# Starting a four-layer graph network kernel: filler products, an earlier flag and an earlier branch

## The chip, the core and the metric

The kernel runs on one core of a Trainium2 chip. A core has a matrix engine (TensorE, PE in the profile; its weight loads are listed as PEld), a vector engine (VectorE, DVE), an activation engine (ScalarE, ACT), a general one (GpSimd, POOL), and SyncE (SP), whose queue here issues all transfers between the chip's main memory and the core's on-chip memory (SBUF). Matrix products land in PSUM, which this kernel divides into eight banks of 128 x 512 fp32. Each engine works through its own list of instructions in order and waits on semaphores for the others.

The metric is device time in microseconds (us), as the median of several runs; smaller is better. One further execution is profiled.

## The reference

There are 32 graphs of 512 nodes with 128 features each, and one 512 x 512 adjacency matrix of zeros and ones that all graphs share. Four layers follow each other, each one of the form x = x + f(relu(layernorm(x))):

```python
# layer 0: attention (h is the normalized input)
x_h = elu(h @ Wi + bi)
e = sigmoid(x_h @ We[H:] [:, :, None] + (x_h @ We[:H])[:, None, :] + be)
e = e * (adj + 0.005 * (adj == 0))
recv = concat([einsum('bij,bjh->bih', e, x_h), x_h * sum(e, -1)]) @ Wn + bn
out = concat([elu(recv), x_h]) @ Wm + bm
# layer 1: five steps of a gated update, with adj as both matrices
m = adj @ h;  z, r = sigmoid(...), sigmoid(...);  h = (1 - z) * h + z * tanh(...)
# layer 2: adj @ (h @ weight) + bias
# layer 3: sum over k of adj^k @ h @ weight_k, up to the third power
```

All values are fp32.

## The kernel before

The kernel is one long list of operations that a planner puts in order before anything runs. `Plan.op` records an operation with its engine, an assumed duration, a due time, the buffers that it reads and writes, and a function that emits its instructions. `Plan.order` then goes through an assumed timeline: whenever an engine comes free it takes the ready operation with the earliest due time, if buffers are free, and if the operation isn't due more than 60 us behind the oldest one left. The emitted order on each engine is what the plan found; the hardware adds the real waits.

Buffers are kinds with slots: "f" (36 tiles of 128 x 512), "q" (4 such tiles in the rounded format fp32r), "s" (small statistics), "x" (input and running sum of four graphs each), "b" (the eight PSUM banks), and "m" and "d" (blocks in main memory, through which token-major and feature-major layouts are exchanged).

A product of fp32 operands is shown in the trace as two matmul records, one of fp32r operands as one. Products with the adjacency matrix can run in fp32r only if rounding leaves every adjacency value unchanged. So the kernel counts the values that rounding changes (`inexact`), reads that count into a register of each engine (L906), and branches (L907) to one of two arms, which hold everything that was not ordered before. In the arm taken here (`arm(True)`), the adjacency `A_r` is fp32r and the tokens are split into two fp32r parts.

What stands before the branch is what `plan.order(end=BRANCH)` places in the first 30 us of its own timeline:

- Loads on SP: graph 0, `Wi`, the four row blocks of the adjacency (`A_nat`), then small weights, biases and graphs 1 to 3 (L279, L295).
- For graph 0 to 3: layer normalization (L434 to L447), PE transposes (L334), the copy out of PSUM (L394), the product with `Wi` (L405, a helper's line), exp, tanh and relu for elu on ACT (L492, L410, L495), its two combining steps on DVE (L497, L499), the products with `W_tok` (L521), attention ends spread by transposes (L558), tanh of each of four tiles (L572) and their masking on DVE (L575), and the products with the messages (L583).
- The adjacency: 16 PE transposes (L464), the rounding copy `A_r` (L466) and a scaled copy (L468) on ACT, the mask (L469) and the comparison of `A_r` with the transposed original (L472) on DVE, which leaves counts in `n_odd`; PE sums these over the partitions (L479), and DVE writes the integer flag `inexact` (L484).

After the branch, SP loads the weights of the later layers; DVE, PE and ACT go on with the first graphs; PE makes the weight transposes (L674) and the adjacency in a permuted order of columns (L757, with a permuted identity called `swap`). Row sums of the masked tiles are taken with a matrix of ones (L405 with `ones`), the node's own part is multiplied in (L609), and layer 0 ends with L619. The later layers' lines are L769 (tokens with adjacency), L405 with w3T, w4T, w5T, u3T, u5T (gates), L833 (layer 2), L850 and L859 (layer 3).

Due times come from constants: each graph begins `PACE` = 56 us after the one before, the first ones by `b * FIRST_PACE` with 10 us; graphs 4 and 5 have due times of 40 and 56.

Of the kernel before, what the change touches and what calls it, by code (L numbers as in the profile page):

```python
# [10 lines left out]
F32 = mybir.dt.float32  # L11
# [5 lines left out]
P = 128  # L17
# [21 lines left out]
class Plan:  # L39
# [7 lines left out]
    def __init__(self, slots, ahead, last):  # L47
        self.ahead, self.last, self.ops, self.vals = ahead, last, [], {}
        self.free = {k: [(0.0, i) for i in range(n)] for k, n in slots.items()}
        self.until = dict.fromkeys(self.RESULT, 0.0)  # L50
        self.shared, self.now = 0.0, 0.0

    def op(self, eng, us, due, emit, reads=(), writes=(), two=False, keep=0, result=None):

        o = Op(eng, us, self.RESULT[eng] if result is None else result, emit, two, keep)
        for v in reads:
            o.before.add(v.writer)  # L60
# [42 lines left out]
    def order(self, end=None):  # L103
# [9 lines left out]
        for i, o in enumerate(left):  # L113
            index[o] = i
            o.waits = sum(not b.begun for b in o.before)
            o.ready = max([0.0, *(self.known(b, o) for b in o.before if b.begun)])
            if not o.waits:
                heapq.heappush(coming[o.eng], (o.ready, i, o))
                events.append(o.ready)
# [16 lines left out]
        while events:  # L136
# [3 lines left out]
            for e in self.until:  # L140
# [12 lines left out]
                for x in passed:  # L153
                    heapq.heappush(ready[e], x)
                if o is None:
                    continue
# [29 lines left out]
def tile_four_graph_layers(  # L186
# [34 lines left out]

    PACE, FIRST_PACE, LAST_PACE = 56.0, 10.0, 30.0
    BRANCH = 30.0

# [25 lines left out]
    def at(v):  # L250
        if v.tile is not None:
            return v.tile
        return places[v.kind][v.slot] if v.whole is None else at(v.whole)[:, v.part]
# [13 lines left out]
    op("POOL", 1.0, -9, lambda: make_identity(nc, at(ident)), [], [ident])  # L267
    op("DVE", 0.2, -9, lambda: nc.vector.memset(at(ones), 1.0), [], [ones])
    op("POOL", 0.2, -9, lambda: nc.gpsimd.memset(at(neg_half), -0.5), [], [neg_half])
    ones_r = const("ones_r", [P, P], F32R)  # L270
# [6 lines left out]

    def load(v, src, due, us=0.5, to=None):
        op("SP", us, due, lambda: nc.sync.dma_start(at(v) if to is None else to(at(v)), src), [], [v])  # L279
        return v  # L280

    def load_const(src, shape, name, due, us=0.5):
        return load(const(name, shape), src, due, us)

# [9 lines left out]
    def load_graph(b, due):  # L294
        op("SP", 1.5, due, lambda: nc.sync.dma_start(  # L295
            at(X[b]), x[b].rearrange("(c p) d -> p c d", p=P)),
            [], [X_group[b // G], X[b]] if b % G == 0 else [X[b]])

    load_graph(0, -9)
    Wi_sb = load_const(Wi, [P, P], "Wi_sb", -9)  # L300
    A_nat = [Val("f") for _ in range(NC)]
    for ic in range(NC):
        load(A_nat[ic], adj[ts(ic, P), :], -8, 1.3)
    bi_sb = load_column(bi, "bi_sb", -8)

# [4 lines left out]
    be_sb = load_const(be.partition_broadcast(P), [P, 1], "be_sb", -7)  # L310
    load_graph(1, -6)
    Wn_sb = load_const(Wn[P:], [P, P], "Wn_sb", -6)
    bn_sb = load_column(bn, "bn_sb", -6)
    Wm_sb = load_const(Wm.rearrange("(t p) o -> p t o", p=P), [P, 2, P], "Wm_sb", -5)
    bm_bc = load_const(bm.partition_broadcast(P), [P, P], "bm_bc", -5)
    load_graph(2, -4)
    load_graph(3, -3)

# [139 lines left out]
    inexact = const("inexact", [1, 1], I32)  # L458
    n_odd = const("n_odd", [P, NC])
    for jc in range(NC):  # L460
        pt, z, odd = Val("b"), Val("f"), Val("f")
        def turn(jc=jc, pt=pt):
            for ic in range(NC):
                nc.tensor.transpose(at(pt)[:, ts(ic, P)], at(A_nat[ic])[:, ts(jc, P)], at(ident))  # L464
        op("PE", T_TR, jc, turn, [*A_nat, ident], [pt])
        op("ACT", T_COPY, jc, lambda jc=jc, pt=pt: nc.scalar.copy(at(A_r)[:, jc, :], at(pt)),  # L466
           [pt], [A_r])
        op("ACT", T_COPY, jc, lambda z=z, pt=pt: nc.scalar.mul(at(z), at(pt), 1 / ALPHA), [pt], [z])  # L468
        op("DVE", T_VEC, jc, lambda jc=jc, z=z, pt=pt: nc.vector.scalar_tensor_tensor(  # L469
            at(mask)[:, jc, :], at(pt), 0.0, at(z), op0=ALU.is_equal, op1=ALU.add),  # L470
            [pt, z], [mask])
        op("DVE", 0.7, 8, lambda jc=jc, pt=pt, odd=odd: nc.vector.scalar_tensor_tensor(  # L472
            at(odd), at(A_r)[:, jc, :].bitcast(F32), 1.0, at(pt),
            op0=ALU.mult, op1=ALU.not_equal, accum_out=at(n_odd)[:, jc : jc + 1]),
            [A_r, pt], [odd, n_odd])
    p_odd = Val("b")
# [169 lines left out]
    assert inexact.writer.begun  # L646
    common = plan.state()

    def arm(exact):
        with ExitStack() as stack:  # L650
            pool = stack.enter_context(tc.tile_pool(name=f"arm{exact:d}", bufs=1))
            plan.back_to(common)
            list_rest(exact, pool)
            issue(plan.order())
# [291 lines left out]
```

## Time and profile before

| what | value |
|---|---|
| median of 3 runs | 1705.13 us (1702.95 to 1705.34) |
| profiled execution | 1704.23 us |
| its span, first to last instruction | 1702.4 us |
| mean granted TensorE clock | 0.996 |
| PE busy | 1665.6 us (98%) |
| DVE busy | 1478.8 us (87%) |
| ACT busy | 1099.6 us (65%) |
| POOL busy | 377.3 us (22%) |

The span is what the trace covers; the execution's time is 1.8 us longer. Busy time is the union of an engine's instructions. Matmuls overlap in the records and their ends are modelled, so a full PE row doesn't say that every matmul runs at its best rate; the distance between starts does. The bracket at the end of a timeline row tells how long the engine had been idle, and what released it. "Issue" there means that the profile shows nothing that it waited for.

### The profile page before, as it was taken

The numbers are of one execution on the slowest core, as the hardware profiler recorded it, in microseconds if no ns is written. First come the engines' busy times: TensorE is split into PE (matmuls) and PEld (weight loads), VectorE is DVE, ScalarE is ACT, GpSimd is POOL, SyncE is SP. The second block draws the span as 40 slices with busy tenths as digits, with TensorE's granted clock in tenths as the row PEclk, the third lists the DMA queues.
The fourth block names the chain that finished last, engine by engine and source line by source line (L and its number), as shares of the span: only waits on it lengthen the run. The fifth ranks groups of instructions, "written<-read, shape, count | busy, mean of one in ns | idle before, by whom it ended". The sixth has DMA issues, their size and how long they took to land.

```text
span 1702.4 us, 21136 instructions
## 1 busy us (share of the span) xinstructions
PE 1665.6 (98%) x6521; PEld 1065.7 (63%) x6521; DVE 1478.8 (87%) x3325; ACT 1099.6 (65%) x2075; POOL 377.3 (22%) x301
## 2 busy tenths in 40 slices
PE   5999999999999999999999999999999999999998
PEld 3565555666666666665666665666666666666787
DVE  5789999999989998889989898899999888877842
ACT  5786767777666776566676666667576756655550
POOL 3231122312312222222212222122232221001210
PEclk8999999999999999999999999999999999999999
DMA  3122323253333332242333333333333323222302
GB/s 95 36 69 93 123 96 99 70 150 92 93 99 112 100 105 88 76 123 93 94 108 91 94 107 87 100 107 107 89 112 95 95 86 101 81 75 75 95 6 62
DMA packets 266873, 156.54 MB, mean 92 GB/s; under 512 B 75392, under 2 KB 235008, under 8 KB 266752
## 3 DMA queue, kind: packets, MB, share of 16 engines
q1 hardware_dynamic: 266752, 155.12, 30.9%
q8 instruction: 53, 0.87, 0.2%
q14 instruction: 68, 0.56, 0.1%
HBM read 82.25 MB, written 72.81 MB: 91 GB/s over the span
## 4 chain that ended last, share of the span: by engine, by line
PE 84%; DVE 8%; DMA 3%; ACT 3%; issue 2%; SPq 0%; POOL 0%; DVEq 0%; ACTq 0%; POOLq 0%
PE b L405 39%; PE b L769 18%; PE b L859 9%; PE b L850 6%; PE b L583 4%; PE b L619 3%; DMA f<-d 2%; PE b L521 2%; DVE f L575 2%; PE b L833 1%; DVE r L743 1%; PE b L606 1%; ACT f L447 1%; DVE f L794 1%; DVE f L346 1%
## 5 line engine op out<-in xcount | busy, mean ns | idle before, releaser
L394 ACT COPY f<-b 128x512 f32<-128x512 f32 x360 | 207.8, 585 | 151.6 <-PE b L769 105.8
L769 PE MATMUL b<-AQ,r 128*128 128x512 f32 x1024 | 304.4, 439 | 0.8 <-DVE r L743 0.8
L439 POOL TENSOR_TENSOR s<-s,nhalf 128x4 f32<-128x4 f32 x128 | 156.0, 1219 | 645.8 <-DVE s L437 610.1
L769 PEld LDWEIGHTS b<-AQ,r 128*128 128x128 f32 x1024 | 192.1, 188 | 90.5 <-issue 49.9
L794 DVE TENSOR_TENSOR f<-f,b 128x512 f32<-128x512 f32 x320 | 211.8, 677 | 20.4 <-PE b L405 16.5
L447 ACT ACTIVATE f<-x,s 128x128 f32<-128x128 f32 x512 | 210.1, 488 | 23.0 <-DVE s L442 22.7
L346 DVE STREAM_TRANSPOSE f<-f 128x512 f32<-128x512 f32 x244 | 204.6, 845 | 22.3 <-ACT f L447 21.7
L859 PE MATMUL b<-r,A_r 128*128 128x512 f32 x768 | 223.6, 426 | 0.0
L410 ACT ACTIVATE f<-f,b4w 128x512 f32<-128x512 f32 x160 | 115.4, 723 | 165.2 <-DVE f L794 164.7
L594 POOL TENSOR_TENSOR f<-f,f 128x512 f32<-128x512 f32 x84 | 130.9, 1559 | 307.3 <-DVE f L575 231.0
L405 PE MATMUL b<-f,u5T 128*128 128x512 f32 x320 | 163.9, 596 | 7.9 <-DVE f L801 7.8
L859 PEld LDWEIGHTS b<-r,A_r 128*128 128x128 f32 x768 | 139.0, 189 | 44.9 <-issue 23.0
L405 PE MATMUL b<-f,w4T 128*128 128x512 f32 x320 | 163.4, 593 | 0.2 <-ACT f L394 0.2
L405 PE MATMUL b<-f,u3T 128*128 128x512 f32 x320 | 163.0, 592 | 0.4 <-DMA f<-m 0.4
L405 PE MATMUL b<-f,w5T 128*128 128x512 f32 x320 | 162.8, 592 | 0.0
L405 PE MATMUL b<-f,w3T 128*128 128x512 f32 x320 | 162.5, 592 | 0.0
L769 PE MATMUL b<-A_r,r 128*128 128x512 f32 x512 | 151.8, 439 | 2.5 <-DVE r L743 2.5
L410 ACT ACTIVATE f<-b,b5w 128x512 f32<-128x512 f32 x160 | 109.2, 684 | 64.5 <-PE b L405 63.5
L743 DVE TENSOR_TENSOR r<-f,r 128x512 fp32r<-128x512 f32 x192 | 143.1, 749 | 8.2 <-ACT r L739 8.1
L850 PEld LDWEIGHTS b<-V,f 128*128 128x128 f32 x1024 | 130.5, 192 | 24.8 <-issue 20.6
L410 ACT ACTIVATE f<-f,b3w 128x512 f32<-128x512 f32 x160 | 115.2, 720 | 42.5 <-DVE f L794 41.6
L811 DVE TENSOR_TENSOR f<-f,f 128x512 f32<-128x512 f32 x160 | 114.7, 718 | 29.3 <-ACT f L410 28.7
(103 smaller groups left out, 2623.8 us busy)
## 6 DMA issues: line engine op xcount, KB each, us to landing
m<-f SPq DMA_DIRECT2D x244, 256.0 KB, 2.1
f<-m SPq DMA_DIRECT2D x184, 256.0 KB, 2.9
f<-m SPq DMA_DIRECT2D x240, 64.0 KB, 2.2
x<-in_x_dram SPq DMA_DIRECT2D x32, 256.0 KB, 3.1
out_dram<-x SPq DMA_DIRECT2D x32, 256.0 KB, 2.4
f<-d SPq DMA_DIRECT2D x28, 256.0 KB, 5.1
f<-in_adj_dram SPq DMA_DIRECT2D x4, 256.0 KB, 4.0
f<-in_L_gnn_weight_dram SPq DMA_DIRECT2D x2, 224.0 KB, 3.3
```

What stands on the lines that cost most here:

```text
L346: op("DVE", us, due, lambda: nc.vector.transpose(view_out(at(blocks)), view_in(at(src))), [src], [blocks])
L394: op("ACT", us, due, lambda: nc.scalar.copy(at(t), at(src)), [src], [t])
L405: nc.tensor.matmul(to, at(w), of, start=start, stop=stop)
L410: op("ACT", us, due, lambda: nc.scalar.activation(at(dst), at(src), AF.Tanh, bias=at(bias), scale=scale), [src, bias], [dst])
L439: op("POOL", 1.2, due, lambda: nc.gpsimd.tensor_tensor(stat(SCALE), stat(VAR), at(neg_half), op=ALU.pow), [s, neg_half], [s])
L447: nc.scalar.activation(at(h)[:, ts(c, P)], at(X[b])[:, c, :], AF.Relu, bias=stat(SHIFT)[:, c : c + 1], scale=stat(SCALE)[:, c : c + 1],)
L594: op("POOL", 1.4, d - 10, lambda: nc.gpsimd.tensor_tensor(at(dst), at(a), at(c), op=ALU.add), [a, c], [dst])
L743: op("DVE", T_VEC, due, lambda: nc.vector.tensor_tensor(part(lo), whole(), part(hi).bitcast(F32), op=ALU.subtract), [src, hi], [lo], two=two)
L769: nc.tensor.matmul(at(pa), at(part)[:, ts(jc, P)], view(at(columns)[:, jc, :]), start=jc == n == 0, stop=jc == NC - 1 and n == PARTS - 1,)
L794: op("DVE", T_VEC, d, lambda: nc.vector.tensor_tensor(at(s), at(u), at(pg), op=ALU.add), [u, pg], [s])
L850: nc.tensor.matmul(at(pz)[:, ts(i, D)], at(hT[i])[:, ts(ic, P)], at(V[k]), start=i == 0, stop=last and i == G - 1,)
L859: nc.tensor.matmul(at(pz), at(adjT)[:, jc, ts(ic, P)], at(part), start=False, stop=jc == NC - 1 and n == PARTS - 1,)
```

## The change

It has seven parts.

1. Filler. One PSUM bank (`spare`) is taken out of the plan up to the branch. Whenever PE has nothing ready on the planned timeline, a 128 x 128 product of `ones` with itself into that bank is emitted. Each is planned at 0.224 us, from 0.4 us on. Nothing reads the bank. After the branch it returns to the plan. The new kernel lists 52 such products: 31 first, then single ones between the adjacency's transposes, 15 behind the first `Wi` product, and 4 more.
2. The flag is counted from the adjacency as loaded: ACT rounds each row block into a "q" tile, and DVE compares that with the block; neither needs the transposes. The number of comparisons stays four.
3. The adjacency's remaining work gets other due times: transposes 8, scaled copies and masks 9 to 12, and the copies `A_r` 22.
4. Loads: graph 1 and `bi` move ahead of the adjacency, graph 2 right behind it, and `bm_bc` isn't issued before the branch. Planned durations of the large loads are smaller.
5. `BRANCH` is 18 in place of 30: fewer operations are placed ahead of the branch.
6. `FIRST_PACE` is 14 in place of 10; graphs 4 and 5 are due at 56 and 70.
7. Ahead of the branch the planner leaves an engine free for an operation that is due earlier and becomes ready within 0.3 of the candidate's duration.

```diff
+                if o is not None and end is not None and any(
+                    c.due < o.due and t < now + 0.3 * o.us for t, _, c in coming[e]
+                ):
+                    heapq.heappush(ready[e], (o.due, index[o], o))
+                    o = None
+                if o is None and e == "PE" and end is not None and self.idle.known <= now:
+                    order.append(self.idle)
+                    self.until[e] = now + self.idle.us
+                    heapq.heappush(events, self.until[e])
...
-    PACE, FIRST_PACE, LAST_PACE = 56.0, 10.0, 30.0
-    BRANCH = 30.0
+    PACE, FIRST_PACE, LAST_PACE = 56.0, 14.0, 30.0
+    BRANCH = 18.0
...
+    spare = places["b"].pop()
+    plan.free["b"].pop()
+    plan.idle = Op("PE", 0.224, 0.0, lambda: nc.tensor.matmul(
+        spare[:, :P], at(ones), at(ones), start=True, stop=True), False, 0)
+    plan.idle.known = 0.4
...
     load_graph(0, -9)
+    load_graph(1, -9)
     Wi_sb = load_const(Wi, [P, P], "Wi_sb", -9)
+    bi_sb = load_column(bi, "bi_sb", -9)
     A_nat = [Val("f") for _ in range(NC)]
     for ic in range(NC):
-        load(A_nat[ic], adj[ts(ic, P), :], -8, 1.3)
-    bi_sb = load_column(bi, "bi_sb", -8)
+        load(A_nat[ic], adj[ts(ic, P), :], -8, 0.65)
+    load_graph(2, -8)
...
-    load_graph(1, -6)
...
-    bm_bc = load_const(bm.partition_broadcast(P), [P, P], "bm_bc", -5)
-    load_graph(2, -4)
-    load_graph(3, -3)
+    bm_bc = load_const(bm.partition_broadcast(P), [P, P], "bm_bc", -5, earliest=BRANCH)
+    load_graph(3, -6)
...
+    for ic in range(NC):
+        short, odd = Val("q"), Val("f")
+        op("ACT", T_COPY, 9, lambda ic=ic, short=short: nc.scalar.copy(
+            at(short), at(A_nat[ic])), [A_nat[ic]], [short])
+        op("DVE", 0.7, 9, lambda ic=ic, short=short, odd=odd: nc.vector.scalar_tensor_tensor(
+            at(odd), at(short).bitcast(F32), 1.0, at(A_nat[ic]),
+            op0=ALU.mult, op1=ALU.not_equal, accum_out=at(n_odd)[:, ic : ic + 1]),
+            [short, A_nat[ic]], [odd, n_odd], two=True)
     for jc in range(NC):
-        pt, z, odd = Val("b"), Val("f"), Val("f")
+        pt, z = Val("b"), Val("f")
...
-        op("PE", T_TR, jc, turn, [*A_nat, ident], [pt])
-        op("ACT", T_COPY, jc, lambda jc=jc, pt=pt: nc.scalar.copy(at(A_r)[:, jc, :], at(pt)),
+        op("PE", T_TR, 8, turn, [*A_nat, ident], [pt])
+        op("ACT", T_COPY, 22, lambda jc=jc, pt=pt: nc.scalar.copy(at(A_r)[:, jc, :], at(pt)),
            [pt], [A_r])
-        op("ACT", T_COPY, jc, lambda jc=jc, pt=pt: nc.scalar.mul(at(z), at(pt), 1 / ALPHA), [pt], [z])
-        op("DVE", T_VEC, jc, lambda jc=jc, z=z, pt=pt: nc.vector.scalar_tensor_tensor(
+        op("ACT", T_COPY, 9 + jc, lambda z=z, pt=pt: nc.scalar.mul(at(z), at(pt), 1 / ALPHA), [pt], [z])
+        op("DVE", T_VEC, 9 + jc, lambda jc=jc, z=z, pt=pt: nc.vector.scalar_tensor_tensor(
             at(mask)[:, jc, :], at(pt), 0.0, at(z), op0=ALU.is_equal, op1=ALU.add),
             [pt, z], [mask])
-        op("DVE", 0.7, 8, lambda jc=jc, pt=pt, odd=odd: nc.vector.scalar_tensor_tensor(
-            at(odd), at(A_r)[:, jc, :].bitcast(F32), 1.0, at(pt),
-            op0=ALU.mult, op1=ALU.not_equal, accum_out=at(n_odd)[:, jc : jc + 1]),
-            [A_r, pt], [odd, n_odd])
...
     common = plan.state()
+    places["b"].append(spare)
...
             plan.back_to(common)
+            plan.free["b"].append((BRANCH, len(places["b"]) - 1))
```

Line numbers in the new kernel differ: L464 becomes L492, L472 becomes L484, L484 becomes L508, L521 becomes L545, L558 becomes L582, L572 becomes L596, L575 becomes L599, L583 becomes L607, L609 becomes L633, L757 becomes L783, L405 becomes L425, and L907 becomes L933. The filler is L285.

## The prediction

> **What bounds the kernel now.** First the page: the span, the busy times, and the rows over 40 slices.
>
> ```profile
> span 1702.4 us, 21136 instructions
> PE 1665.6 (98%) x6521; PEld 1065.7 (63%) x6521; DVE 1478.8 (87%) x3325; ACT 1099.6 (65%) x2075; POOL 377.3 (22%) x301
> PE   5999999999999999999999999999999999999998
> PEclk8999999999999999999999999999999999999999
> ```
>
> TensorE is the bound: it idles 36.8 us in 1702.4, and one slice, the first, is half empty and below full clock. Second, busy time by stage, cut where TensorE becomes continuous (47.35) and where its last matmuls begin. Columns: stretch, length, then PE, PEld, DVE, ACT, POOL busy with counts, granted clock, DMA share, GB/s.
>
> ```profile
> 0.00:47.35 47.35, 28.64 (x108) 17.76 (x109) 25.54 (x99) 29.07 (x62) 16.31 (x27) 0.86 0.31 85
> 47.35:1697.10 1649.75, 1636.58 (x6414) 1047.94 (x6413) 1451.82 (x3226) 1070.49 (x2014) 360.96 (x274) 1.00 0.31 92
> 1697.10:1702.40 5.30, 0.40 (x2) 0.00 (x0) 1.42 (x3) 0.00 (x0) 0.00 (x0) 0.97 0.51 148
> ```
>
> Idle: 18.7 at the start, 13.2 in the whole middle, 4.9 at the end. Finer cuts show the clock:
>
> ```profile
> 15.00:16.00 1.00, 0.00 (x0) 0.00 (x0) 0.47 (x1) 1.00 (x4) 1.00 (x1) 0.96 0.00 0
> 20.00:25.00 5.00, 4.39 (x24) 3.38 (x24) 1.87 (x9) 2.63 (x7) 1.64 (x2) 0.50 0.00 2
> 29.00:30.00 1.00, 1.00 (x3) 0.53 (x2) 0.00 (x0) 1.00 (x3) 0.95 (x1) 0.71 1.07 320
> ```
>
> Half speed runs from 15.9 to 29.6, and at the very start too, where no grant is recorded: the adjacency transposes take 0.213 each (3.41 for 16), later ones 0.11. Third, the timeline around the branch:
>
> ```profile
> 20.61 2.10 PE L521 MATMUL b<-W_tok,f 128*128 128x130 f32 x8 [7.46 <-DVE f L499]
> 23.36 0.14 DVE L484 CAST inexact<-b 1x1 int32<-1x1 f32 x1
> 32.39 0.69 DVE L497 SCALAR_TENSOR_TENSOR f<-f,f 128x512 f32<-128x512 f32 x1 [4.03 <-issue]
> 34.22 1.12 PE L583 MATMUL b<-f,f 128*128 128x512 f32 x2 [2.16 <-DVE f L499]
> ```
>
> The flag is written at 23.4-23.5. PE's branch instruction (L907) stands at 29.61 for 4.55 us; its next matmul starts at 34.22, though the DVE result that it needs was done at 28.35. DVE passes its branch at 28.10 and resumes at 32.39 (4.3), ACT takes 3.4 from its branch, and SP 3.66 from the flag to its next DMA (23.52 to 27.18).
>
> Now the work done in that start at full speed, with durations from later rows (0.43 per 128x512 fp32 record, two to a product; 0.11 per 128x128 or 128x130 record; 0.23 per 128x512 fp32r record). Before 47.35: 37 transposes by 0.11 and 8 of the attention ends (4.9 together), 4 Wi products 3.4, 24 W_tok records 2.6, eight L583 records 3.4, eight ones records 3.4, Wn 0.9, swap 0.9, count 0.2: about 19.9. So **27.4 us are lost by 47.35**: 18.7 idle, about 6.7 by half clock (13.4 busy us at half rate), 2 in small gaps. What follows is the same TensorE work in both kernels.
>
> **What the skill says.** "TensorE: Matmul & The Clock Gate", Part 1: the gate's default is half rate, and free-running windows of about 3.4 us decide. The trace agrees: full at 12.5, half from 15.9, full from 29.6, so steps of 3.41 and 13.65. A window with 0.65 busy of 3.41 lost the clock; one with about 2.2 kept it. "Runtime: NRT & Kernel Launch", Instruction fetch mechanics: a taken branch outside the fetched pages waits for a fetch; that fits the 3.4 to 4.6 us above. "Advanced Engine Details and Errata", Control Flow Timing, gives 0.108 us for a compare-and-branch; the trace's 4.55 decides.
>
> **The change, part by part**, in the order that the two built programs list.
>
> 1. Filler: 52 products of ones, 31 of them first (they need only the memset of ones, done at 0.98). Each has two 128x128 records: 0.223 at full clock, 0.43 at half. Starting at 1.1, the clock should rise after one fully busy window, at 4.5 to 7.9 by phase, say 6.2: 12 slow, 19 fast, so they end at 1.1 + 5.1 + 4.2 = 10.4 (9.6 to 11.2). They are queued ahead of the adjacency transposes, whose data land earlier: graph 1 goes ahead of the adjacency, whose last issue moves from 3.2 to about 4.1, plus 4.2 to landing = 8.3. So up to 2 us is held back on the path; it is counted in the times below.
>
> 2. Graph 0. Two adjacency blocks (0.9) to 11.3, filler, x transposes to 12.0, two more blocks, filler, Wi product 13.1-13.95 (ACT's copy is done at 12.65). ACT makes three mask inputs, then exp, tanh, relu at 0.57-0.6 each, to 16.2. DVE finishes elu at 17.0, so 15 fillers (3.35, to 17.3) cost 0.3. W_tok products end at 18.2. Before: they began at 20.61.
>
> 3. Flag. ACT now rounds the adjacency as loaded, during filler; the four comparisons no longer need A_r. DVE's last comparison ends at 17.65, the count on PE at 18.4; on DVE a mask, a score and another mask stand between (17.6 to 19.1), so the flag is at 19.3, 4.2 sooner. Two of the four A_r copies move behind the branch; what needs them, the swap products, stands some 30 TensorE instructions (over 10 us) later, so they cost nothing; without that cover they would cost 1.2.
>
> 4. Branch. SP's first DMA goes out at 19.3 + 3.66 = 23.0. In SP's queue bm_bc moves from before the branch to first behind it, landing at 23.0 + 3.9 = 26.9. POOL's bias additions, 1.26 each, wait for it, and the swap's copy on POOL is queued behind three of them, about 33.5; the swap products come at about 38, so it is hidden by 4 us. The weight loads start at about 24 instead of 28.3. Graph 5's load moves from second behind the branch to behind the eleven weight loads, about 23 + 7 (as these took before) + 3.4 = 33.4; DVE's statistics of it stand ahead of graph 0's product with the row sum (L633), which PE wants at 36 to 37: hidden by 1 to 2 us, and every us beyond that would show. DVE reaches the branch at 21.1 and resumes at 25.3. On PE the last wait before it is the second Wi product: ACT copies 20.3, PE 20.4-21.3; the load of the flag 20.4, the branch 21.0, next matmul at 25.6. Its first matmul needs a masked tile from DVE: 25.3 + 0.7 = **26.0**. Nothing but the first masked tile can run then: everything on PE is queued behind it. Idle 21.3 to 26.0 = 4.7, where before it was 2.2, because there six L583 records were already queued.
>
> 5. Lost time in after's start. Work by 26.0: 16 + 8 transposes and 4 ends 3.1, two Wi 1.7, eight W_tok records 0.9, count 0.2 = 5.9; lost 20.1. Then either (a) the clock falls in the 4.7 us gap. Two windows of 3.41 cover it with 2.1 busy between them, so one has at most 1.1 busy, between the two observed cases but nearer the one that fell; regaining it takes 3.4 to 6.8 us of half rate, 1.7 to 3.4 lost, say 2.4, and later waits hide under the slow matmuls but for 0.5: lost **23.0**. Or (b) it stays: 0.5 waiting for graph 2's transposes (ACT: three exponents, exp, tanh, relu, A_r, normalization, 24.9 to 30.8) and 1.0 for weight copies as before (0.4 + 0.3 + 0.3): lost 21.6.
>
> 6. First pace 14 for 10, later due times for graphs 4 and 5 (40 to 56, 56 to 70), and the order of everything after: no TensorE work is added, so it costs nothing while TensorE stays covered; bounds -4 to +10, from the 13.2 us idle and about 10 us of small gaps in the middle.
>
> Sum for (a): 23.0 - 27.4 = -4.4 on the profiled execution's 1704.2 us (span 1702.4 and 1.8 around it) = 1699.8; the median of the runs is 0.9 above, so **1700.7**.
>
> **Rivals.** (b) The clock stays up, or the middle runs a little better: -5.8 to -8, about 1698. For it: a window with 2.2 busy kept the clock; against: 4.7 idle is twice what was survived. (c) The head start is eaten: TensorE reaches the covered middle earlier, but waits there for other engines (DVE is 88% busy in the middle) and for row gathers through memory; about 1704, within 0.2%. (d) Slower: the reordered middle starves TensorE more. Place: stretches such as 400 to 450, where PE was busy 47.5 of 50 behind DVE and DMA round trips. Price: about 2 us per such stretch; from 4 more than now (4.4 + 3.4 = 7.8 us) it ends slower, at about 1710. Against: no instruction was added there. (e) The filler doesn't raise the clock or its 31 products at half rate end at 14.4 instead of 10.4, so that the path slips 4 and everything cold adds 3: about 1705 to 1708; a tail of (c) and (d).
>
> **How the numbers follow.** (a) 0.46, own range 1697.5 to 1703.7, two thirds of it below 1701.7; (b) 0.20; (c) 0.20; (d) 0.14. 0.2% (3.4 us) is about what a measurement of this kernel can tell from no change: faster is below 1701.7: 0.46 x 0.68 + 0.20 = 0.51; same 0.46 x 0.32 + 0.20 = 0.35; slower 0.14. The range 1694 to 1709 leaves out the far ends of (b) and (d).
>
> **What would show it.** Right: filler from about 1.1, full clock granted before 8; L492 transposes at 0.11 each from about 10.4; the flag (L508) near 19.3; SP's next DMA near 23; PE's first L607 near 26.0 after an idle of 4 to 5 with the clock at half somewhere in 25 to 32; PE continuous after; middle idle near 13. Wrong: filler at 0.43 throughout, a flag later than 21, the first L607 after 28, or a middle idle above 18.

## The result and the profile after

The changed kernel takes 1706.92 us (median of 20 runs, 1704.04 to 1711.3) where the kernel before takes 1703.90 on the same chip: a ratio of 1.0017 (95% interval 1.0009 to 1.0025). That is 3 us slower, within the 0.2% that a measurement of this kernel can hardly tell from no change, but its interval leaves out the forecast gain of 4.4 us. The direction was wrong. The stated range held the time, but at 15 us it is wide enough to hold no change at all. (The forecast of 1700.7 was also built on three runs of before with a median of 1705.13; 20 runs put that 1.2 lower.)

The profiled execution of after took 1709.51 us (span 1707.7), 2.6 above the median; that of before lies 0.3 above its own. Of what follows, some 2.3 us is therefore that one execution's own.

The page of after: span, busy times, and the slices of TensorE and its clock.

```profile
span 1707.7 us, 21318 instructions
PE 1678.7 (98%) x6625; PEld 1075.7 (63%) x6625; DVE 1481.4 (87%) x3325; ACT 1100.4 (64%) x2079; POOL 381.5 (22%) x301
PE   8999999999999999999999999999999999999998
PEclk9999999999999999999999999999999999999999
```

TensorE's busy time grew by 13.1 us: the 104 filler records alone are busy for 14.7. Only the first slice, now fuller and with a higher granted clock, looks different from before.

The timeline of the start (start, length, engine, line, operation; in brackets the idle before it and its releaser):

```profile
1.03 9.14 PE L285 MATMUL b<-ones 128*128 128x128 f32 x62 [1.03 <-DVE ones L280]
10.01 1.04 PE L492 MATMUL b<-ident,f 128*128 128x128 f32 x8
16.85 1.06 PE L545 MATMUL b<-W_tok,f 128*128 128x130 f32 x8
18.71 0.14 DVE L508 CAST inexact<-b 1x1 int32<-1x1 f32 x1
22.32 0.35 SPq L298 DMA_DIRECT2D bm_bc<-in_L_gnn_bm_dram  x1
24.20 3.65 DVE L599 SCALAR_TENSOR_TENSOR f<-f,mask 128x512 f32<-128x512 f32 x4 [3.89 <-issue]
24.95 4.54 PE L607 MATMUL b<-f,f 128*128 128x512 f32 x6 [3.95 <-DVE f L599]
```

This is the start as the prediction drew it: the filler ends at 10.0, the flag is cast at 18.7, the first product behind the branch starts at 24.95 where before it started at 34.22. The busy table by stage (stretch, length, then PE, PEld, DVE, ACT, POOL busy with counts, granted clock, DMA share, GB/s) shows the rest of the answer:

```profile
49.47:1702.40 1652.93, 1634.00 (x6381) 1043.28 (x6380) 1449.41 (x3221) 1064.41 (x2002) 363.93 (x273) 1.00 0.31 92
...
25.00:30.00 5.00, 5.00 (x9) 2.21 (x10) 5.00 (x8) 5.00 (x11) 3.96 (x5) 0.66 0.60 148
...
300.00:350.00 50.00, 47.70 (x175) 28.60 (x174) 49.60 (x113) 37.35 (x75) 16.78 (x13) 1.00 0.31 92
```

TensorE idles 18.9 us in the middle, against 13.2 before. In 300 to 350, VectorE is busy 49.6 of 50 us and TensorE idles 2.3; before, TensorE was busy for the whole of that stretch, with VectorE at 49.76.

**Lost time at equal work.** Since both kernels do the same TensorE work behind the branch, the two traces are best compared at equal work, not at equal times. For every TensorE record the full-speed work that stands ahead of it is added up (0.429 us per 128x512 fp32 record, 0.2305 per fp32r record, 0.1113 per 128x128 or 128x130 record; filler counts as nothing). The record's start minus that sum is the time lost so far, good to about half a us.

| work done, us | 75 | 150 | 250 | 350 | 500 | 700 | 900 | 1100 | 1300 | 1640 |
|---|---|---|---|---|---|---|---|---|---|---|
| before | 27.1 | 27.6 | 29.5 | 29.7 | 37.5 | 40.0 | 41.9 | 44.8 | 47.9 | 50.2 |
| after | 21.9 | 24.4 | 27.5 | 32.3 | 35.3 | 40.8 | 46.7 | 49.0 | 54.8 | 55.5 |

After is 5.2 us ahead once the start is over, has lost it all by work 350, is ahead again at 500, and is 5.3 behind at the end, which is the difference of the two spans. The start gave 5.2 and the middle took 10.5, about 8 if what the two profiled executions took beyond their medians lies in the middle. Below, "start" is the loss at work 75 and "middle" the loss from there to 1640.

What TensorE waited for in before, with the total in us, the number of waits and the longest (rows of the middle):

```profile
PE b L405 <- DVE f L801: 7.8, 7, 1.9
...
PE b L769 <- DVE r L743: 3.3, 2, 2.5
...
PE b L583 <- DVE f L575: 1.0, 1, 1.0
```

The same view of after:

```profile
PE b L607 <- DVE f L599: 8.1, 9, 4.0
PE b L425 <- DVE f L827: 7.7, 7, 1.9
PE b L630 <- DVE q L625: 3.0, 4, 1.2
PE b L795 <- DVE r L769: 2.0, 2, 1.2
```

All of these waits end with a result of VectorE. The 7.7 us at L425 is the same as before (L405). New in the middle are masked tiles (L607: eight waits and 4.1 us besides the 4.0 at the branch, before 1.0) and L630 (3.0, not in the list before). Idle time explains 5.7 of the 10.5 us.

But the engine named in these rows is not always the one that is late. Ahead of seven of the eight waits for masked tiles (3.7 of the 4.1 us) VectorE was itself idle, waiting for ScalarE, and ScalarE was idle for a transfer, as here (rows from the timeline of all engines):

```profile
581.34 2.56 ACT L596 ACTIVATE f<-f,s 128x512 f32<-128x512 f32 x4 [0.99 <-DMA f<-d]
...
582.10 3.60 DVE L599 SCALAR_TENSOR_TENSOR f<-f,mask 128x512 f32<-128x512 f32 x4 [2.64 <-ACT f L596]
...
582.85 1.55 PE L607 MATMUL b<-f,f 128*128 128x512 f32 x3 [0.41 <-DVE f L599]
```

The transfer (`f<-d`, L572) reads a graph's attention ends back from main memory into a whole tile; this one was issued at 575.13 and landed at 581.32. The page of after lists all 28 of them (KB each, median us from issue to landing; before has 5.1, and 2.9 is what after's other reads of 256 KB, `f<-m`, take):

```profile
f<-d SPq DMA_DIRECT2D x28, 256.0 KB, 5.3
```

The planner counts on 4.05 (0.45 for the issue and 3.6 until the tile is there), and on 7.1 from the end of the row's transposition on VectorE to the landing; in after that whole way takes 8.0 in the median and up to 9.7. Followed back in this way, TensorE's waits in the middle come to 12.8 us behind a VectorE that was busy right up to the awaited tile and 3.7 us behind transfers; in before to 9.5 and 1.4.

Another 1.7 us of the loss comes from one hole deep enough to cost TensorE its clock:

```profile
850.00:855.00 5.00, 3.05 (x11) 1.80 (x10) 4.97 (x16) 2.86 (x6) 1.02 (x1) 1.00 0.24 81
855.00:860.00 5.00, 5.00 (x16) 3.31 (x15) 2.64 (x6) 2.75 (x7) 0.00 (x0) 0.66 0.10 27
```

TensorE is idle 1.95 us up to 854.55 while VectorE is busy 4.97 of 5; half speed for some 3.4 us follows. (It need not happen in every run: 13 of the 20 have a mean granted clock of 0.998 or 0.999 against 0.997 in this execution, and average 1705.9 us, the other seven 1708.7. So at least part of this 1.7 belongs to the 2.3 us that are this execution's own.) The remaining 3 us are recorded neither as idle nor as half clock.

### The profile page after: what moved, and what is told of

It reads as the page before. It is cut to its first block, busy times and chain, and to the rows that moved or that the text cites. A ratio compares the mean times of both kernels' runs of the same rounds, so it can differ in the third digit from the quotient of the medians.

```text
span 1707.7 us, 21318 instructions
## 1 busy us (share of the span) xinstructions
PE 1678.7 (98%) x6625; PEld 1075.7 (63%) x6625; DVE 1481.4 (87%) x3325; ACT 1100.4 (64%) x2079; POOL 381.5 (22%) x301
## 4 chain that ended last, share of the span: by engine, by line
PE 76%; DVE 13%; DMA 5%; ACT 3%; issue 2%; SPq 0%; DVEq 0%; ACTq 0%
PE b L425 35%; PE b L795 16%; PE b L885 9%; PE b L876 6%; DMA f<-d 4%; PE b L607 3%; PE b L643 3%; DVE f L599 3%; DVE r L769 1%; PE b L545 1%; DVE f L366 1%; DVE f L820 1%; PE b L859 1%; ACT f L596 1%; DVE f L841 1%
## 5 line engine op out<-in xcount | busy, mean ns | idle before, releaser
L618 POOL TENSOR_TENSOR f<-f,f 128x512 f32<-128x512 f32 x84 | 132.9, 1583 | 291.2 <-DVE f L599 186.8
L425 PE MATMUL b<-f,u5T 128*128 128x512 f32 x320 | 164.3, 598 | 7.7 <-DVE f L827 7.7
L885 PEld LDWEIGHTS b<-r,A_r 128*128 128x128 f32 x768 | 139.2, 189 | 47.3 <-issue 25.4
L425 PE MATMUL b<-f,w4T 128*128 128x512 f32 x320 | 163.2, 593 | 0.0
L425 PE MATMUL b<-f,u3T 128*128 128x512 f32 x320 | 162.7, 592 | 0.0
L425 PE MATMUL b<-f,w5T 128*128 128x512 f32 x320 | 162.3, 592 | 0.0
L425 PE MATMUL b<-f,w3T 128*128 128x512 f32 x320 | 161.9, 592 | 0.0
L769 DVE TENSOR_TENSOR r<-f,r 128x512 fp32r<-128x512 f32 x192 | 140.8, 738 | 12.6 <-ACT r L765 12.2
L837 DVE TENSOR_TENSOR f<-f,f 128x512 f32<-128x512 f32 x160 | 108.9, 682 | 29.6 <-ACT f L430 29.2
```

Of the source, the lines that this page charges most:

```text
L425: nc.tensor.matmul(to, at(w), of, start=start, stop=stop)
L618: op("POOL", 1.4, d - 10, lambda: nc.gpsimd.tensor_tensor(at(dst), at(a), at(c), op=ALU.add), [a, c], [dst])
L769: op("DVE", T_VEC, due, lambda: nc.vector.tensor_tensor(part(lo), whole(), part(hi).bitcast(F32), op=ALU.subtract), [src, hi], [lo], two=two)
L885: nc.tensor.matmul(at(pz), at(adjT)[:, jc, ts(ic, P)], at(part), start=False, stop=jc == NC - 1 and n == PARTS - 1,)
```

## The experiments

The theory after this comparison: the new order of the rest makes TensorE wait for VectorE and costs more than the start gains. The rivals: the first pace of 14 is at fault; any order would have eaten the gain; or the filler's warm clock is worth less than thought. All ratios below are to the kernel before on the same chip, with their 95% interval.

### 1. The start and the rest exchanged

The listing for before and for after stands in one kernel. A first pass only lists the order of one; the second emits the start (up to the branch) of the other and then all remaining operations in the sequence of the first, with buffer slots handed out oldest first (lines left out are marked):

```diff
+    def follow(self, tags):
+        by_tag = {o.tag: o for o in self.ops if not o.begun}
+        order = [by_tag[t] for t in tags if t in by_tag]
...
+        for n, o in enumerate(order):
...
+            o.begun = True
+            for v in o.takes:
+                v.slot = self.free[v.kind].pop(0)[1]
...
-            issue(plan.order())
...
+                after = plan.follow(rest[exact])
...
+                issue(after)
```

> The changed start (filler, early flag, early branch), then the remaining operations in the sequence in which the kernel before has them. If the order of the rest ate the gain: the start still loses about 5 us less, the middle loses what it loses in the kernel before (13 us idle), so about 1699 us, ratio 0.997. If VectorE, full from 150 to 350, eats any head start whatever the order: the middle loses 3 to 5 us more than before, 1703 to 1705, ratio 1.000. If the way the start ends (which banks and buffers are free, which weights are late) does the harm: 1706 to 1708, ratio 1.002.

> The start of the kernel before, then the remaining operations in the sequence of the changed kernel. If the order of the rest ate the gain: 8 us more in the middle and nothing won at the start, about 1712 us, ratio 1.005. If VectorE eats any head start: the head start was worth nothing, so 1704 to 1707, ratio 1.000 to 1.002. If the way the changed start ends does the harm: 1703 to 1705, ratio 1.000.

| start | rest | median, us | ratio | start lost | middle lost |
|---|---|---|---|---|---|
| before | before | 1704.6 | 1 | 27.1 | 23.1 |
| after | before | 1703.68 | 0.9991 [0.9981, 1.0000] | 22.0 | 27.5 |
| before | after | 1712.12 | 1.0044 [1.0031, 1.0056] | 25.4 | 27.5 |
| after | after | 1706.92 | 1.0017 [1.0009, 1.0025] | 21.9 | 33.6 |

From the 64th record on (filler not counted), TensorE and VectorE show in both exchanged kernels exactly the sequence of operations that the second column names. The new order of the rest costs 0.44%, 7.5 us, when the start is the old one. The new start takes 0.27%, some 4.6 us, off that (0.12 to 0.42% by the two intervals), about what was forecast for it; but under the old order of the rest it is worth only 0.09% (1.5 us by the ratio, 0.9 by the medians), and the interval reaches to no gain. (The profiled execution of the third row lies 5.3 us below its median, so its middle of 27.5 understates. A rest of another order also differs in what of its waits falls before work 75, which may be why the starts read 25.4 and 27.1 with the same listing up to the branch.) So the new start with the old rest came out as the second case of its expectation, the old start with the new rest as the first of its own, and neither theory stands alone: the order is worse, and a head start is also eaten under the old one. (No kernel was run that follows its own order in this way, so what slots handed out oldest first cost by themselves is not known.) In the second row the head start of 5 us lasts until work 900 (37.5 lost there, before 41.9) and goes at 1000 to 1125. The windows of that kernel at that place:

```profile
1050.00:1055.00 5.00, 3.07 (x12) 1.89 (x11) 4.97 (x16) 3.40 (x6) 1.02 (x1) 1.00 0.29 97
1055.00:1060.00 5.00, 5.00 (x16) 3.17 (x15) 2.64 (x6) 2.22 (x5) 0.00 (x0) 0.66 0.03 7
```

It is the same sort of hole as after's at 850: VectorE full, TensorE idle for 1.9 us, then the clock at half. The head start goes here, not between 150 and 350 us, where the expectation had placed it.

### 2. The first pace, and the pace of all graphs

First the one constant of the planner that the change sets anew, put back in after and put forward in before:

```diff
-    PACE, FIRST_PACE, LAST_PACE = 56.0, 14.0, 30.0
+    PACE, FIRST_PACE, LAST_PACE = 56.0, 10.0, 30.0
```

> The changed kernel with the first graphs' pace back at 10 (graphs 4 and 5 due at 40 and 56 again). If the later due times of the first graphs make the bad order: about 1699 us, ratio 0.997. If any new plan of the rest comes out some us better or worse without a rule: anywhere in 1699 to 1712, with the loss in other places than in the changed kernel. If VectorE eats the head start: 1703 to 1706.

> The kernel before with the first graphs' pace at 14. If the later due times make the bad order: 8 us more, about 1712 us, ratio 1.005. If any new plan comes out better or worse without a rule: 1700 to 1712. If the earlier branch (the plan of the rest starts at 18 in place of 30) makes it: 1703 to 1705, ratio 1.000.

After with 10 takes 1.0034 [1.0021, 1.0047], some 3 us more than after itself, though the intervals just overlap; before with 14 takes 1.0063 [1.0049, 1.0078]. The pace isn't the culprit in after, since putting it back gains nothing. (With 10 its start loses 25.1 us instead of 21.9: the half clock behind the branch lasts 6.8 us there instead of 3.4.) But in before the same 4 us of due time cost 11 us, which raised the question of how far any change of order scatters the time. So the pace of all later graphs was moved by 0.1 us (55.9 and 56.1 for 56.0). Nothing in the start's order changes by that, but a large part of the order behind the branch does.

> The kernel before with the planner's steady pace at 55.9 in place of 56: the start is the same, about 1000 of TensorE's instructions of the rest change places. No work and no rule changes. If the middle of the kernel before is an ordinary outcome of its planner: 1702 to 1707, ratio 0.999 to 1.001. If it is an unusually good one, so that almost any new order of the rest costs what the changed kernel's did: 1708 to 1716, ratio 1.002 to 1.007.

> The same with 56.1. Ordinary outcome: 1702 to 1707. Unusually good one: 1708 to 1716.

> The changed kernel with the steady pace at 55.9. If new orders of the rest scatter without a rule: 1702 to 1712, and the mean of the changed kernel's three paces stands 4 to 6 us below the mean of the three paces of the kernel before, which is the head start. If something in the changed kernel makes its middle bad whatever the order: 1706 to 1709, and no gap between the two means.

> The same with 56.1. Scatter: 1702 to 1712, head start shown in the means. A fixed cost in the changed kernel: 1706 to 1709.

| pace | before | after |
|---|---|---|
| 55.9 | 1.0051 [1.0037, 1.0064] | 0.9996 [0.9988, 1.0004] |
| 56.0 | 1 | 1.0017 [1.0009, 1.0025] |
| 56.1 | 1.0007 [0.9998, 1.0015] | 1.0064 [1.0050, 1.0078] |
| mean, us | 1707.2 | 1708.0 |

A pace shifted by 0.2% moves the time by -4 to +9 us, with no rule to be seen in the sign. The expectation that orders scatter held. The other half, that after's three paces would lie 4 to 6 us below before's on average because of the head start, did not: the means are 0.8 apart, the other way, though three orders each are too few to see 4 us in a scatter of 9 to 12. What they do show is that before's own order is a good draw among its neighbours: 1703.7 beside 1712.6, 1705.5 and the 1715.8 of pace 14.

The middle accounts for it each time: it loses 32.7 us in before at 55.9, 22.7 at 56.1, and in after 23.6 at 55.9 and 36.0 at 56.1. The busy table of the stretch from 60 to 1650 in before:

```profile
60.00:1650.00 1590.00, 1576.83 (x6096) 999.45 (x6095) 1429.68 (x3184) 1052.95 (x1979) 358.41 (x272) 1.00 0.32 93
```

The same stretch in before at pace 55.9:

```profile
60.00:1650.00 1590.00, 1570.64 (x6027) 990.63 (x6026) 1438.50 (x3178) 1051.13 (x1973) 366.29 (x272) 1.00 0.32 93
```

TensorE gets through 69 records fewer in the same time, while VectorE is busier by 9 us and GpSimd by 8 for six VectorE operations fewer. So here the same operations take VectorE longer; experiment 5 returns to that. It is no mark of a slow order, though: in the same stretch VectorE is busy 1426.2 us in after itself, with 6031 TensorE records, and 1437.2 in the faster after at 55.9, with 6099.

A last combination, the new start with the old rest at pace 56.1:

> The changed start, then the sequence of the kernel before at pace 56.1 (1705.5 us with its own start; its middle lost 22.7 us in its profile). If a head start is kept by some orders: 1700 to 1702, ratio 0.998. If an order fits only the start for which it was planned: 1703.5 to 1707, ratio 1.000 to 1.001.

0.9999 [0.9990, 1.0007], 1703.5 us, against 1705.5 for the old start with that rest. Its loss at work 75 is 25.1, so most of the head start is not even there by then. The two ratios' intervals overlap, so the 2 us between them are no more than suggested.

### 3. The filler taken out

```diff
-                if o is None and e == "PE" and end is not None and self.idle.known <= now:
+                if False and o is None and e == "PE":
```

> The changed kernel without the filler products, every other instruction in the same order. If the filler is what pays at the start by keeping the clock up: the adjacency transposes run at 0.21 each, the clock is at half up to about 30, the start loses 1.5 to 3 us more, so 1708 to 1710. If the earlier flag and branch alone make the head start, or the 31 products hold up what they warm: 1705 to 1707, the start's loss within 1 us of the changed kernel's.

Timeline of TensorE in that kernel:

```profile
6.45 1.05 PE L492 MATMUL b<-ident,f 128*128 128x128 f32 x2 [6.45 <-DMA f<-in_adj_dram]
16.27 2.10 PE L545 MATMUL b<-W_tok,f 128*128 128x130 f32 x8 [2.88 <-DVE f L523]
25.17 4.54 PE L607 MATMUL b<-f,f 128*128 128x512 f32 x6 [2.73 <-DVE f L599]
```

1.0014 [1.0004, 1.0024], 1705.7 us: no slower than with filler. TensorE starts its transposes at 6.45 instead of 10.01, does the W_tok records in twice the time (2.10 for eight, 1.06 with filler), and still begins the first product behind the branch only 0.22 us later. The start lost 22.3 us, with filler 21.9. Up to the branch ACT and VectorE set the pace, and half-speed TensorE hides behind them. What the full clock still wins, the filler in part takes back: it holds TensorE's own work up, so that the W_tok products begin at 16.85 instead of 16.27. So the gain of the start comes from the other parts of the change; what shows of them is the earlier flag and branch (parts 2 to 7 were not taken apart, but for the first pace). The hole at 850 with its half clock stands in this trace too.

### 4. VectorE made lighter

To see whether the middle is lost to VectorE, one VectorE operation, which runs 160 times, is cut from 512 to 32 columns. The kernels leave out that part of the computation; no order, wait or other operation changes. First the last of three that follow each other (L815 before, L841 after), then three (L811, L813 and L815, and their like in after):

```diff
-                    at(c), at(c), 0.5, at(h), op0=ALU.mult, op1=ALU.add), [c, h], [c], two=True)
+                    at(c)[:, :32], at(c)[:, :32], 0.5, at(h)[:, :32],
+                    op0=ALU.mult, op1=ALU.add), [c, h], [c], two=True)
```

> The kernel before, its order untouched, with one VectorE operation of layer 1 (the last blend of each of 160 steps) done on 32 of 512 columns; the other columns keep the unblended value. That takes some 0.5 us from VectorE 160 times, about 80 us of 1479, and nothing from TensorE. If TensorE's losses in the middle come from VectorE having no slack: the middle loses 5 to 10 us where it lost 23, so 1686 to 1692. If they come from transfers or from TensorE itself: 1700 to 1704.

> The changed kernel with the same VectorE operation cut to 32 of 512 columns. If VectorE's lack of slack makes the middle's losses: the middle loses the same 5 to 10 us as in the kernel before so lightened, and the head start of about 5 us shows: 1681 to 1687, 4 to 6 us below it. If the losses come from something else: 1703 to 1707, still above the lightened kernel before.

> The kernel before with pace 55.9 (9 us slower than with 56), lightened in the same way. VectorE's slack as the cause: within 2 us of the lightened kernel before. Otherwise: still 7 to 9 us above it.

> The changed kernel with pace 56.1 (7 us slower than with 56), lightened in the same way. VectorE's slack as the cause: within 2 us of the lightened changed kernel. Otherwise: still 5 to 8 us above it.

> The kernel before with all three VectorE operations that end a step of layer 1 (difference, product, blend) done on 32 of 512 columns; the other columns keep the value of the new state before blending. About 240 us less on VectorE, the same on TensorE. If VectorE makes all of the middle's loss: the middle loses under 6 us (23 in the kernel before, 12 with one operation cut), so 1682 to 1688. If other waits hold the rest: 1690 to 1693.

> The changed kernel with the same three operations cut. If VectorE makes all of the middle's loss: the head start of 5 us shows whole, 1677 to 1683, 4 to 6 us below the kernel before so cut. If other waits hold the rest: 1686 to 1692, and within 3 us of it.

| cut | kernel | median, us | ratio | start lost | middle lost |
|---|---|---|---|---|---|
| one | before | 1693.20 | 0.9936 [0.9919, 0.9953] | 26.4 | 12.2 |
| one | after | 1692.66 | 0.9922 [0.9905, 0.9938] | 21.9 | 17.4 |
| one | before, 55.9 | 1699.16 | 0.9962 [0.9948, 0.9976] | 26.4 | 19.0 |
| one | after, 56.1 | 1700.67 | 0.9976 [0.9964, 0.9987] | 22.4 | 22.8 |
| three | before | 1688.48 | 0.9913 [0.9896, 0.9930] | 26.4 | 8.0 |
| three | after | 1685.92 | 0.9895 [0.9879, 0.9911] | 22.0 | 8.9 |

No TensorE work was taken away, and yet each kernel gains 11 to 14 us from the one cut and 15 to 21 from three. So most of the middle's loss goes, in both kernels, when VectorE has less to do. (A cut operation is also a link in the chain of its own step; what its earlier result brings and what the freed time brings were not told apart.) One cut did less than expected: the middle still loses 12.2 and 17.4 us, not 5 to 10, and the changed kernel is ahead by 0.5 us instead of 4 to 6. With three cut, when the middle loses 8 or 9 us in both, the changed kernel is ahead by 2.6 us: 1685.9 against 1688.5 (their intervals against before overlap, but the four runs of each, on one chip, lie apart: 1684.86 to 1686.46 and 1687.97 to 1690.84). That is the forecast's direction and a good half of its 4.4 us. It is not the whole head start of 4 to 6 us, which was expected if VectorE made all of the loss, but the case in which other waits hold the rest. The longest of TensorE's waits in after with three cut:

```profile
PE b L607 <- DVE f L599: 6.0, 5, 3.9
```

L425's 7.7 us and L630's 3.0 are gone, and 3.9 of the 6.0 is the branch itself. The scatter between orders did not fall to the 2 us that was expected with one cut: pace 55.9 is still 6 us behind before and 56.1 8 us behind after. The order still counts when VectorE has some 77 us less to do.

### 5. GpSimd's additions made shorter

While a GpSimd addition of 128x512 runs, a VectorE operation with two inputs in SBUF is recorded at about 1.75 us instead of 0.68, as here in after, shortly before its hole (the timeline of all engines):

```profile
845.61 0.68 DVE L839 SCALAR_TENSOR_TENSOR f<-f,f 128x512 f32<-128x512 f32 x1
...
845.83 3.27 POOL L618 TENSOR_TENSOR f<-f,f 128x512 f32<-128x512 f32 x2 [0.70 <-DVE f L599]
...
846.21 1.75 DVE L769 TENSOR_TENSOR r<-f,r 128x512 fp32r<-128x512 f32 x1
...
847.88 1.77 DVE L841 SCALAR_TENSOR_TENSOR f<-f,f 128x512 f32<-128x512 f32 x1
...
854.55 1.59 PE L425 MATMUL b<-f,u5T 128*128 128x512 f32 x2 [1.95 <-DVE f L827]
```

Two additions run from 845.83 to 849.10. L769 and L841, with two SBUF inputs each, take 2.2 us more than they need. VectorE is then busy without a break until it finishes L827 at 854.5, for which TensorE has been waiting for 1.95 us.

The Trainium skill describes this: "SBUF — State Buffer", section "🔬 SBUF: two separate sides", says that the two engines share a pair of ports under an exclusive lock, and that the loser is blocked for the whole of the other's instruction, a VectorE operation with two SBUF inputs being concerned when GpSimd reads SBUF. The trace agrees: L839, which starts ahead of the additions, takes 0.68. Of the VectorE operations of 128x512 that start in after while one of these additions runs, 41 of the 57 with two SBUF inputs take over 1.5 us, but none of the 31 with an input in PSUM takes over 0.9. The planner knows of this: on its timeline a VectorE operation marked `two` and one on GpSimd never overlap (`shared`); in the run they drift together all the same.

There are 43 such long operations (over 1.5 us) in before (46 us above 0.68 each in all), 49 in after (53; 26 of the 49 are the masking, L599), 60 in before at 55.9 (63), 53 in after at 55.9 (56) and 53 at 56.1 (57). The rival theory was that the new order simply runs into this lock more often. The additions (L594, L618; 84 of them) were cut to 32 columns, which leaves out most of that sum in both kernels:

```diff
-                    at(dst), at(a), at(c), op=ALU.add), [a, c], [dst])
+                    at(dst)[:, :32], at(a)[:, :32], at(c)[:, :32], op=ALU.add), [a, c], [dst])
```

> The kernel before with the 84 GpSimd additions of layer 0's masked tiles done on 32 of 512 columns, so that the row sums of graphs 4 to 31 are not the reference's; order and every other instruction the same. GpSimd gets about 110 us less. If these additions, by holding up VectorE, make much of the middle's loss (23 us): half of it or more goes, 1690 to 1694. If VectorE's own work makes it: 1700 to 1704.

> The changed kernel with the same additions cut to 32 of 512 columns. If they make much of the middle's loss (34 us in the profile, 31 by the median): 1688 to 1693. If VectorE's own work makes it: 1702 to 1706.

Before so cut takes 1688.35 (0.9908 [0.9892, 0.9925], middle 7.5), after 1690.83 (0.9920 [0.9904, 0.9937], middle 15.7). The page of before with short additions:

```profile
PE 1661.0 (98%) x6521; PEld 1067.3 (63%) x6521; DVE 1433.9 (85%) x3325; ACT 1101.3 (65%) x2075; POOL 288.8 (17%) x301
```

VectorE's busy time falls by 45 us (from 1478.8), about the 46 us of excess counted above, and the kernel gains 16, about as much as by cutting three VectorE operations, which took 223 us off VectorE. For each us of VectorE's busy time that is five times as much, though both cuts leave a middle of about 8, below which neither may be able to go. (A shorter addition also delivers its own result sooner; that share was not told apart.)

But the lock alone does not explain why after is behind before. With most of it out of the way (3 long operations are left in before, 7 in after) after is still 2.5 us slower (the four runs of each lie apart) and its middle loses 8 us more, about 7 after allowing for the profiled executions. After at 55.9 has as many long operations as after at 56.1 and is 12 us faster. Its waits with short additions:

```profile
PE b L607 <- DVE f L599: 10.2, 10, 3.9
PE b L425 <- DVE f L827: 1.3, 2, 0.7
```

The waits at L425 are nearly gone; those for masked tiles are not, and 6.3 us of them are in the middle. Of these, eight waits with 5.9 us end in the transfer `f<-d`, with VectorE idle, as at 581.34 above; in before with short additions it is three with 1.7 us. So some 4 of the 7 to 8 us that its middle loses more here belong to the way of the attention ends through main memory, not to VectorE's load. This is read from the traces: no run changed the transfer or its due time.

## Why the prediction was wrong

Its numbers, by step, beside after's trace:

| step | forecast | measured |
|---|---|---|
| 1, filler ends | 10.4 (9.6 to 11.2) | 10.0 |
| 2, W_tok products end | 18.2 | 17.9 |
| 3, flag | 19.3 | 18.7 to 18.85 |
| 4, SP's next DMA; first L607 | 23.0; 26.0 | 22.3; 24.95 |
| 4, idle before L607 | 4.7 | 3.95 |
| 5, lost in the start | 23.0, before 27.4 | 21.9, before 27.1 |
| 6, order of everything after | 0 (-4 to +10) | about +8 (+10.5 in the profiled executions) |

**Steps 1 to 5 held.** Each event came 0.3 to 1.1 us earlier than worked out, and the clock fell in the gap at the branch as in case (a): half from 25.6 to 29.05. The head start was 5.2 us, forecast 4.4. What step 1 got wrong is only what the filler is for: its times are right, but the kernel without it is as fast (1705.7 against 1706.9), because W_tok and the flag wait for ACT and VectorE anyway. Rival (e) took 3 us for a cold start; it cost 0.4.

**Step 6 failed**: "the order of everything after: no TensorE work is added, so it costs nothing while TensorE stays covered". The value taken, 0, was wrong, and the bound of +10 about right. TensorE does not stay covered. With VectorE busy 1450 of 1650 us, a listing in another order makes some L827 late behind it, or some masked tile behind its transfer (TensorE's waits behind a busy VectorE grew from 9.5 to 12.8 us, those behind transfers from 1.4 to 3.7), and the four or so us that the start gains are no more than what a mere change of order moves (-4 to +9 for 0.1 us of pace). The same step overlooked that a cover this thin also eats a head start when the order of the rest does not change: 5 us became about 1 in the first experiment.

**The rivals.** What happened is (c) and (d) together. (d) named the right mechanism, a reordered middle that starves TensorE behind VectorE and memory round trips, and its deciding point of 7.8 us; about 8 came. Its argument against, "no instruction was added there", carries no weight: none was added in before at pace 55.9 either. (c) pointed at VectorE at 88% in the middle and at row gathers through memory, and the run with three operations cut bears out the first: with VectorE's load down from 87 to 74% of the span, the forecast gain shows in part (-2.6 us). (b) and (e) did not happen.

**What stays open.** Which trait of an order makes it good is not known. The runs show that before's order is a good one among five, and the traces that masked tiles (L599) are late in after, even with GpSimd's additions cut, because their transfer lands late. Whether the new due times leave that transfer too little room, and what a longer planned time for it would bring, was not tried. Nor was the lock's cost separated from that of the later sums.

## What to carry to other kernels

A head start on the bounding engine is a gain only if the next busiest engine has the slack to follow; here, at 87% busy in a static order, it had not: under the old order 5 us became about 1. When a wait names an engine, look whether that engine was busy or itself waiting: here some two fifths of what the waits grew by ended in a transfer. Before crediting a reordering, or blaming it, move one irrelevant constant of the planner by a little and see how far the time moves: here by up to 9 us, more than the effect in question. And look for operations on an engine off the path that lengthen those of a busy one: cutting 84 additions on an engine 22% busy took 16 us off.

## What the hardware showed that was not expected

- A VectorE operation of 128x512 with two SBUF inputs takes 0.68 us alone and about 1.75 beside a GpSimd addition of the same size, one with an input in PSUM no longer than alone; cutting 84 such additions to 32 columns took 16 us off 1704.
- The clock falls within a dense stream after a single hole: 1.95 us idle before 854.55 in after, and half speed for some 3.4 us behind it. The same was seen in new start with old rest at 1055. The place counts as well as the length. The recorded clock changes in steps of 3.41 us; over all traces of this case it was lost after every step in which TensorE was busy for less than 1.47 us, and after none with more than 1.62. In after the step of the hole holds 1.46; in before a hole of 1.94 us before 1058.69 left the clock up, and its step holds 1.71.
- The branch stops the engines for different times. TensorE's instruction is shown in the query for that line (operation; duration in ns least, middle, most; first and last start); VectorE's and ACT's are recorded at 0.08 and 0.05 us, and yet VectorE's next work starts at 24.20 and ACT's at 24.16, 3.4 and 3.5 us after their branches at 20.8 and 20.7.

```profile
L933 PEldq COMPARE_BRANCH  x1: 4272/4272/4272, 20.3 to 20.3; - x1
L933 ACTq COMPARE_BRANCH  x1: 45/45/45, 20.7 to 20.7; - x1
L933 DVEq COMPARE_BRANCH  x1: 76/76/76, 20.8 to 20.8; - x1
```
